# The second expert's weight load and the routing steps: another queue and another order

## The chip, the cores and the metric

One core of one Trainium2 chip runs the whole kernel. The metric is the device time of one launch in microseconds (us); lower is better.

## The reference

The input is 1024 tokens of 1024 channels, float32. A first layer adds a convolution-like attention with group norm. A second layer adds a 16-head causal attention and then a mixture of experts; the change lies in this last part. A layer norm is taken of every token, a gate picks experts, and each expert is one 1024 x 1024 product:

```python
gate_logits = softmax(x @ gate_w + gate_b, axis=-1)
selected = (gate_logits >= THRESHOLD)              # 0.1, 8 experts
weights = gate_logits * selected
weights = weights / where(sum(weights) == 0, 1, sum(weights))
for e in range(E):
    out = out + weights[:, e:e + 1] * (x @ expert_w[e] + expert_b[e])
```

What is returned is the token stream plus this sum.

## The kernel before

The tokens are eight tiles of 128 rows (`NT = 8`). The experts don't multiply every token: for each expert the kernel makes a list of the tokens that chose it, gathers their rows, multiplies them, scales them and adds them to the output with an accumulating DMA. Two experts, 0 and 7, are called short: for these the last tile of tokens isn't listed but multiplied in full, expert 0's share at the start ("the dense tile") and expert 7's at the end.

**Grouping, beside the attention's output projection.** The projection (`project_out`, L894) works through nine half tiles, each of eight products over 128 channels. After every product it calls `one_more` (L1373), which counts a "chunk" and issues the steps that the table `at_chunk` (L1326) lists for it. So the table is an order written out by hand: it says which small step follows which product. A step is `stage(n, t)` (L1306) for tile t:

- 0 `normalise` (L1116): layer norm of the rows; for tiles 0 to 5 the rows go to DRAM (L1129) and come back in quarters (L174), both by SP's queue.
- 1 `turn_rows` (L1139): VectorE transposes the quarters (L179); tiles 6 and 7 are transposed by TensorE (L1148) and copied by ScalarE (L1149).
- 2 `gate_sums` (L1158): TensorE products with the gate's weights (L1164), and a copy (L1168).
- 3 `gate` (L1174): products pg (L1179), maximum, exponential on ScalarE (L1191, L1194).
- 4 `thresholds` (L1197): ten small VectorE steps.
- 5 `place` (L1212): running counts `kept` (L1217), products pp (L1219, L1220), the place of each token (L1224 to L1230).
- 6 `entries_of` (L1233): comparisons `one` on VectorE (L1237) and products `entry` (L1245), which GpSimd makes for tiles 0 to 5 and VectorE for 6 and 7.
- 7 `enter` (L1254): TensorE products that add the entries to the lists (L1256).

Stages 2 to 5 run for a group of tiles at once: (0, 1, 2), (3, 4, 5), (6), (7). Each engine issues its steps in the order of the code inside such a stretch, so a step that waits holds back all later ones of its engine. The second table, `others` (L1364), holds what hangs on chunk numbers without being a stage; at chunks 43 and 65 ScalarE's queue loads the halves of expert 0's weights (`w0`).

**The dense tile and expert 0.** `weighted` (L1018) multiplies the last tile by expert 0's weights: two halves of eight products each (L1025), an addition of the bias on VectorE (L1028) and a scale on ScalarE (L1029). Its table `between` says what is issued after product (j, c), and after half j before that half's bias addition. In it come the last tile's stages 2 to 5, the transposes `put` of the gathered rows (L1457, L179), their sums `row_sums` (L1468, L152 to L155) and the sums of the weights, `first_sum` to `fourth_sum` (L1428 to L1442). GpSimd fetches rows by indirect DMA, four per row tile (`fetch`, L1006; L1010).

Then follows a loop over the experts (L1592). It loads the next expert's weights at its top (`load`, L1422: two halves of 2 MB by SP's queue, L121), and calls `products` (L1473) twice per expert, each for a pair of row tiles. That is a matrix product with seven block products in place of eight (L1487), numbered 0 to 6, with VectorE additions between them (L1495 to L1507). Its `between` hangs steps on these numbers. For expert 0, the last tile's stages 6 and 7 hang on product 2, `copy_lists` on 3 (L1264), and `last_lists` on 4 (L1400): products pc that spread the lists (L1276) and copies of them for all other experts (L1295 to L1298).

PSUM banks come from two sets of three, `mm` and `tr`; a product into a bank waits until its last content has been read.

Of the kernel before, what the change touches and what calls it, by code (L numbers as in the profile page):

```python
# [45 lines left out]
NT = TOK // P  # L46
# [10 lines left out]
E = 8  # L57
# [12 lines left out]
def kernel(  # L70
# [27 lines left out]
    nc = tc.nc  # L98
# [896 lines left out]
    w_even, t_pool = pool(weights, "w_even", 2), pool(weights, "t_pool")  # L995

    def half_weights(e, r, home, name="w_e", queue=nc.sync):

        return w_tile(f"{name}{e}_{r}", expert_w[e][:, ts(r, HALF)], home=home, queue=queue)
# [67 lines left out]
    with ExitStack() as gating:  # L1067
# [238 lines left out]
        def stage(n, t):  # L1306
            tiles = together[t]
            if n == 0:
                normal[t] = normalise(t)
            elif n == 1:  # L1310
                turned_rows[t] = turn_rows(t, normal[t])
            elif n == 2:
                summed[t] = gate_sums(tiles)
            elif n == 3:
                gated[t] = gate(tiles, summed[t])
            elif n == 4:
                gated[t] = thresholds(*gated[t])
            elif n == 5:
                placed[t] = place(tiles, *gated[t])
            elif n == 6:  # L1320
                entered[t] = entries_of(t, t - tiles[0], *placed[tiles[0]])
            else:
                enter(t, *entered[t])
# [6 lines left out]
            23: ((1, 1),),  # L1330
            27: ((0, 3),),
            30: ((1, 2),),
            33: ((2, 0),),
            34: ((0, 4),),
            36: ((3, 0),),
            38: ((1, 3), (4, 0)),
            42: ((5, 0), (6, 0)),
            44: ((6, 1),),
            46: ((7, 0), (6, 2)),
            47: ((1, 4),),  # L1340
            48: ((7, 1),),
            50: ((0, 5),),
            52: ((7, 2),),
            61: ((1, 5),),
            63: ((2, 3),),
            65: ((0, 6),),
            66: ((3, 3),),
            68: ((4, 3),),
            69: ((1, 6),),
            71: ((2, 6), (5, 3), (6, 3)),  # L1350
            73: ((3, 6), (6, 4)),
            75: ((7, 3), (4, 6), (6, 5)),
            76: ((7, 4),),
            77: ((5, 6), (6, 6)),
# [64 lines left out]
        w_odd, two = pool(pairs, "w_odd", 2, side="right"), pool(pairs, "two", 2, side="right")  # L1419
        w, bias, step, T, T3, A, S = {0: w0}, {0: bias0[0]}, {}, {}, {}, {}, {}  # L1420

        def load(e):  # L1422
            w[e] = [half_weights(e, r, w_odd if e % 2 else w_even) for r in range(2)]

        def half(e, j, l):
            return w[e][l][:, 4 * j : 4 * j + 4, :]
# [5 lines left out]
        def second_sum(e):  # L1432
            nc.vector.tensor_sub(T[e][1], half(e, 1, 1), T[e][0])  # L1433

        def bias_step(e):
            step[e] = two.tile([P, HALF], F32, tag="step", name=f"step{e}", bufs=1)
            nc.vector.tensor_sub(step[e], bias[e][:, HALF:], bias[e][:, :HALF])

        def fourth_sum(e):
            nc.vector.tensor_sub(T[e][2], half(e, 1, 0), T[e][1])  # L1440
# [16 lines left out]
        def put(e, k):  # L1457

            if k == last:
                A[e, k] = l2w.tile([P, NC, P], F32, tag="row_T", name=f"one{e}", bufs=3)  # L1460
                turn(A[e, k], row[e, k], LEFT)
            else:
                pair, i = divmod(k, 2)
                if i == 0:
                    A[e, pair] = two.tile([P, 2, NC, P], F32, tag="A", name=f"A{e}_{pair}")
                turn(A[e, pair][:, i, :, :], row[e, k])

        def row_sums(e, pair):  # L1468
            S[e, pair] = two.tile([P, 3, NC // 2, P], F32, tag="S", name=f"S{e}_{pair}")
            blocks = (A[e, pair][:, i, 4 * j : 4 * j + 4, :] for i in range(2) for j in range(2))  # L1470
            sums_of_A(*blocks, *(S[e, pair][:, i, :, :] for i in range(3)))
# [89 lines left out]
        with tc.manual_schedule():  # L1561
            entries, last_rows = [], []
            last_row_T = two.tile([P, NC, P], F32, tag="last_row_T", name="last_row_T", bufs=1)
            nc.scalar.copy(last_row_T, turned_rows[NT - 1])
            for k in range(3):
                get(0, k)
            y = weighted(
                lambda: gated[NT - 1][0][:, 0, 0, 1:2],
                turned_rows[NT - 1],
                w0,  # L1570
                bias0[0],
                l2w,
                "dense",
                {
                    (0, 2): lambda: stage(2, NT - 1),
                    (0, 4): lambda: (stage(3, NT - 1), first_sum(0)),
                    (0, 6): lambda: stage(4, NT - 1),
                    0: lambda: put(0, 0),
                    (1, 2): lambda: stage(5, NT - 1),
                    (1, 3): lambda: put(0, 1),  # L1580
                    1: lambda: (row_sums(0, 0), second_sum(0), bias_step(0)),
                },
            )
            get(0, 3)
            nc.gpsimd.indirect_dma_start(
                out=out,
                out_offset=bass.IndirectOffsetOnAxis(ap=token_i[:, NT - 1 : NT], axis=0),
                in_=y,
                in_offset=None,
                compute_op=ALU.add,  # L1590
            )
            for e in range(E):  # L1592
                if e % 2 == 0 and e:
                    left_over(e)
                if e + 1 < E:
                    load(e + 1)
                between = {
                    0: lambda: third_sum(e),
                    1: lambda: put(e, 2),
                    2: lambda: put(e, 3),  # L1600
                    4: lambda: row_sums(e, 1),
                }
                if e == 0:
                    between[2] = lambda: (stage(6, NT - 1), stage(7, NT - 1), fourth_sum(0), put(0, 2))
                    between[3] = lambda: (entries.append(copy_lists(1)), put(0, 3))
                    between[4] = lambda: last_lists(entries[0])
                    between.pop(1)
                elif e % 2:
                    between[0] = lambda: (third_sum(e), get(e, 3))
                    between[1] = lambda: (fourth_sum(e), put(e, 2))  # L1610
                if e % 2 == 0:
                    between[5] = lambda: (get(e + 1, 0), row_sums(0, 1) if e == 0 else None)
                    between[6] = lambda: get(e + 1, 1)
                elif e + 1 < E:
                    between[5] = lambda: (get(e, last), get(e + 1, last))
                    between[6] = lambda: get(e + 1, 0)
                products(e, 0, between)
                if e + 1 < E:
                    bias[e + 1] = expert_bias(e + 1, l2w, tag="xg", bufs=2)
                    between = {  # L1620
                        4: lambda: first_sum(e + 1),
                        5: lambda: second_sum(e + 1),
                        6: lambda: bias_step(e + 1),
                    }
                if e % 2 == 0:
                    between[1] = lambda: (put(e + 1, 0), get(e + 1, 2))
                    between[2] = lambda: put(e + 1, 1)
                    between[3] = lambda: row_sums(e + 1, 0)
                elif e + 1 < E:
                    between[1] = lambda: put(e, last)  # L1630
                    between[2] = lambda: (put(e + 1, last), sum_left(e))
                    between[3] = lambda: (put(e + 1, 0), get(e + 1, 1))
                else:
                    between = {
                        1: lambda: nc.sync.dma_start(last_rows[0], out[ts(NT - 1, P), :]),
                        4: lambda: nc.vector.scalar_tensor_tensor(
                            last_rows[0], bias[e], gated[NT - 1][0][:, 0, e, 1:2], last_rows[0], ALU.mult, ALU.add
                        ),
                    }
                products(e, 1, between)  # L1640


            for j in range(2):
                pe = mm(f"last_pe{j}")
                for c in range(NC):
                    nc.tensor.matmul(
                        pe, last_row_T[:, c, :], w[E - 1][j][:, c, :], start=(c == 0), stop=(c == NC - 1)
                    )
                y = last_rows[0][:, ts(j, HALF)]
                nc.vector.scalar_tensor_tensor(y, pe, gated[NT - 1][0][:, 0, E - 1, 1:2], y, ALU.mult, ALU.add)  # L1650
                nc.sync.dma_start(out[ts(NT - 1, P), ts(j, HALF)], y)
# [69 lines left out]
```

## Time and profile before

| | us |
|---|---|
| median of 3 runs | 1237.42 |
| lowest and highest run | 1237.3, 1238.69 |
| the profiled execution's own time | 1237.59 |
| its span, first to last instruction | 1235.8 |
| of it, to the start of the grouping | about 664 |
| grouping, to the dense tile's first product | 664 to 746.5 |
| dense tile | 746.5 to 761.3 |
| expert 0 | 761.3 to 809.6, and its last products to 816 |
| other experts and the end | to 1235.8 |

The profile is one execution, taken by the hardware profiler. PE is TensorE's matmul, PEld its weight load, DVE VectorE, ACT ScalarE, POOL GpSimd, SP the engine that issues most DMAs; a "q" behind an engine's name marks its sequencer, which issues DMAs. A float32 product shows as two matmuls. A row of the timeline gives start, duration, engine, line, operation, what is written and read, how often, and in brackets how long the engine had been idle before and what ended that. A list of waits gives who waited for whom, the total, the number of times and the longest. A DMA's own row is its issue; the trace also has the time at which its data landed. The granted TensorE clock was 1.000 throughout.

### The profile page before, as it was taken

The page shows a single profiled execution, that of the slowest core. Times are in us where ns is not written, and L with a number is a line of the kernel's source. Part 1 is how long each engine was busy: PE and PEld are TensorE (multiplying, and loading weights), DVE is VectorE, ACT ScalarE, POOL GpSimd, SP SyncE. Part 2 cuts the span into 40 slices and gives each one's busy share as a digit, 9 for nine tenths or more (in the row PEclk, how much of TensorE's full clock was granted, in tenths as well). Part 3 has the DMA queues.
Part 4 walks back from the last instruction along what each step waited for, and adds up shares of the span by engine and source line. Part 5 has one row for each costly group of instructions (what it writes and reads, how often), then busy time and mean ns, then how long its engine had stood idle before and what let it go on. Part 6 is the DMA issues. An engine that isn't in the chain of part 4 may idle for free.

```text
span 1235.8 us, 13219 instructions
## 1 busy us (share of the span) xinstructions
PE 1216.3 (98%) x4780; PEld 630.9 (51%) x4780; DVE 730.6 (59%) x1254; ACT 208.1 (17%) x502; POOL 410.1 (33%) x470
## 2 busy tenths in 40 slices
PE   9999999999999999999999999899999999999998
PEld 5445885778884444444444444444344434434443
DVE  5796636657333666657554656666656556565642
ACT  3310111120001222222221122101201111111110
POOL 0041341354000322223241116436452745364521
PEclk9999999999999999999999999999999999999999
DMA  9002014772210535353393747473855575556442
GB/s 349 23 1 80 6 50 140 240 254 69 68 47 23 167 107 166 105 172 103 114 291 113 232 171 255 88 219 89 239 146 155 111 230 164 147 143 180 100 83 54
DMA packets 94120, 169.76 MB, mean 137 GB/s; under 512 B 11968, under 2 KB 48848, under 8 KB 94048
## 3 DMA queue, kind: packets, MB, share of 16 engines
q1 hardware_dynamic: 75680, 112.68, 28.1%
q0 software_dynamic: 16144, 51.45, 17.3%
q10 hardware_dynamic: 2224, 4.72, 1.1%
q8 instruction: 39, 0.64, 0.2%
q14 instruction: 33, 0.27, 0.1%
HBM read 116.12 MB, written 48.50 MB: 133 GB/s over the span
## 4 chain that ended last, share of the span: by engine, by line
PE 67%; issue 13%; DMA 6%; POOL 6%; DVE 4%; SPq 2%; ACT 1%; DVEq 0%; POOLq 0%; ACTq 0%
PE p L1487 30%; PE pv L657 7%; POOL s_q L855 5%; PE pq_pair L392 4%; PE po L898 3%; PE left L1529 3%; PE pq L311 3%; PE pqk L657 3%; PE pk L423 2%; DMA ln_rows<-ln_rows 2%; PE pv L530 2%; PE rest L1543 2%; PE pT L502 2%; DMA quarters<-rows 1%; SPq L174 1%
## 5 line engine op out<-in xcount | busy, mean ns | idle before, releaser
L1010 POOL DMA_INDIRECT w_e_xg<-rows,gather x146 | 157.3, 1077 | 50.9 <-issue 41.1
L1487 PE MATMUL p<-w_e,A 128*128 128x512 f32 x368 | 163.2, 593 | 1.3 <-DVE slot L1297 1.3
L855 POOL TENSOR_TENSOR s_q<-s_q,total 128x128 f32<-128x128 f32 (+1 forms) x128 | 66.2, 548 | 276.8 <-DVE total L852 274.4
L1033 POOL DMA_INDIRECT out_dram<-y,add x32 | 57.4, 1795 | 177.3 <-ACT y L1493 111.1
L898 PE MATMUL po<-w_p,y_T 128*128 128x512 f32 x256 | 115.8, 601 | 0.0
L1487 PEld LDWEIGHTS p<-w_e,A 128*128 128x128 f32 x368 | 69.6, 190 | 89.9 <-issue 89.4
L1487 PE MATMUL p<-T,S 128*128 128x512 f32 x256 | 112.8, 593 | 0.4 <-DVE T L1433 0.4
L1493 ACT ACTIVATE y<-y,slot 128x512 f32<-128x512 f32 x64 | 46.0, 721 | 339.9 <-DVE y L1501 181.2
L841 ACT ACTIVATE s_q<-s,top 128x256 f32<-128x256 f32 (+1 forms) x128 | 56.6, 443 | 186.4 <-issue 147.0
L657 PE MATMUL pqk<-ln,w_qk 128*128 128x512 f32 x192 | 85.6, 595 | 0.0
L1487 PEld LDWEIGHTS p<-T,S 128*128 128x128 f32 x256 | 48.5, 190 | 61.6 <-issue 60.3
L898 PEld LDWEIGHTS po<-w_p,y_T 128*128 128x128 f32 x256 | 46.8, 190 | 52.3 <-issue 51.1
L179 DVE STREAM_TRANSPOSE A<-w_e_xg 128x1024 f32<-128x1024 f32 x32 | 39.7, 1239 | 52.4 <-DMA w_e_xg<-rows,gather 52.4
L657 PE MATMUL pqk<-T,S_qk 128*128 128x512 f32 x128 | 58.5, 599 | 0.0
L657 PEld LDWEIGHTS pqk<-ln,w_qk 128*128 128x128 f32 x192 | 36.0, 190 | 43.3 <-issue 42.3
L1487 PE MATMUL p<-T,A 128*128 128x512 f32 x128 | 57.5, 592 | 0.0
L1487 PE MATMUL p<-w_e,S 128*128 128x512 f32 x128 | 57.5, 592 | 0.0
L657 PE MATMUL pv<-w_v,ln 128*128 128x256 f32 x192 | 43.7, 380 | 2.3 <-ACT ln L215 1.1
L311 PE MATMUL pq<-w_q,xn 128*128 128x512 f32 x96 | 44.5, 599 | 0.3 <-ACT xn L291 0.3
L1529 PE MATMUL left<-w_e,one 128*32 128x512 f32 x312 | 41.8, 593 | 0.0
L657 PEld LDWEIGHTS pv<-w_v,ln 128*128 128x128 f32 x192 | 36.2, 190 | 7.9 <-ACT ln L215 1.3
L1487 PEld LDWEIGHTS p<-T,A 128*128 128x128 f32 x128 | 24.3, 190 | 30.6 <-issue 30.1
(328 smaller groups left out, 1849.9 us busy)
## 6 DMA issues: line engine op xcount, KB each, us to landing
w_e<-in_expert_w_dram SPq DMA_DIRECT2D x14, 2048.0 KB, 12.1
s_rows<-s_q SPq DMA_DIRECT2D x32, 384.0 KB, 2.3
s_rows<-s_rows SPq DMA_DIRECT2D x128, 96.0 KB, 2.4
w_qk<-in_W_attnT_dram SPq DMA_DIRECT2D x8, 1024.0 KB, 5.9
xn<-in_xT_dram SPq DMA_DIRECT2D x8, 512.0 KB, 7.2
w_q<-in_Wq_dram SPq DMA_DIRECT2D x16, 256.0 KB, 6.8
x_at<-in_x_dram POOLq DMA_DIRECT2D x8, 512.0 KB, 8.2
w_v<-in_W_attnT_dram SPq DMA_DIRECT2D x2, 2048.0 KB, 10.0
```

Of the source, the lines that this page charges most:

```text
L179: nc.vector.transpose(row_T[:, :, :slots].rearrange("p c (g j) -> p g c j", j=32), row[:, : slots // 32, :].rearrange("p g (c i) -> p g c ...
L311: nc.tensor.matmul(pq, xn[:, c, ts(t, P)], w_q[kc][:, c, :], start=(c == 0), stop=(c == NC - 1))
L392: nc.tensor.matmul(bank, a[:, c, :], b[:, c, :], start=(c == 0), stop=(c == NC // 2 - 1))
L657: nc.tensor.matmul(bank, stationary(c), moving(c), start=(c == 0), stop=(c == NC // 2 - 1))
L841: nc.scalar.activation(blocks(h, qt), s[:, h, cols].rearrange("p (b f i) -> p b f i", f=Q, i=32), AF.Exp, bias=top[:, qt, h : h + 1], accu ...
L855: nc.gpsimd.tensor_mul(blocks(h, qt), blocks(h, qt), total[:, qt, h : h + 1].unsqueeze(2).unsqueeze(3).to_broadcast([P, 1 + qt, Q, 32]),)
L898: nc.tensor.matmul(po, y_T[:, c, ts(t, P)], w_p[j][:, c, :], start=(c == 0), stop=(c == NC - 1))
L1010: nc.gpsimd.indirect_dma_start(out=row[:, g, :], out_offset=None, in_=table[: (TOK - P) * Q, :] if e in SHORT else table, in_offset=bass.I ...
L1033: nc.gpsimd.indirect_dma_start(out=out[: TOK - P, :] if e in SHORT else out, out_offset=bass.IndirectOffsetOnAxis(ap=add[:slots, e, k : k ...
L1487: nc.tensor.matmul(bank, a[:, c, :], b[:, c, :], start=(c == 0), stop=(c == NC // 2 - 1))
L1493: nc.scalar.mul(y[i][:, ts(j, HALF)], y[i][:, ts(j, HALF)], slot[:, e, 1, 2 * pair + i : 2 * pair + i + 1])
L1529: nc.tensor.matmul(bank[ts(i, 32), :], stationary, w[of][j][:, c, :], start=(c == 0), stop=(c == NC - 1))
```

## The change

Three things move; no step is added or removed.

1. `load` gets a parameter for the queue. Expert 1's weights are no longer loaded at the top of the loop by SP; they are loaded by ScalarE's queue, in the dense tile's step list after its second half's products (ahead of that half's bias addition and scale). The later experts' loads stay at the top of the loop, on SP.
2. The last tile's stage 5 follows the dense product (1, 1) instead of (1, 2), and its stage 6 comes with it instead of after expert 0's product 2.
3. In `at_chunk`, the stages of the two groups of three tiles and their neighbours come one or two chunks later, with some orders inside a chunk changed by that.

```diff
         at_chunk = {
...
-            33: ((2, 0),),
             34: ((0, 4),),
-            36: ((3, 0),),
-            38: ((1, 3), (4, 0)),
-            42: ((5, 0), (6, 0)),
-            44: ((6, 1),),
-            46: ((7, 0), (6, 2)),
+            35: ((2, 0),),
+            38: ((1, 3), (3, 0)),
+            40: ((4, 0),),
+            44: ((5, 0), (6, 0)),
+            46: ((6, 1),),
             47: ((1, 4),),
-            48: ((7, 1),),
-            50: ((0, 5),),
-            52: ((7, 2),),
+            48: ((7, 0), (6, 2)),
+            50: ((7, 1), (0, 5)),
+            53: ((7, 2),),
             61: ((1, 5),),
-            63: ((2, 3),),
-            65: ((0, 6),),
-            66: ((3, 3),),
-            68: ((4, 3),),
-            69: ((1, 6),),
-            71: ((2, 6), (5, 3), (6, 3)),
-            73: ((3, 6), (6, 4)),
+            65: ((2, 3), (0, 6)),
+            68: ((3, 3),),
+            69: ((4, 3), (1, 6)),
+            71: ((2, 6),),
+            72: ((5, 3), (6, 3)),
+            74: ((3, 6), (6, 4)),
             75: ((7, 3), (4, 6), (6, 5)),
...
-        def load(e):
-            w[e] = [half_weights(e, r, w_odd if e % 2 else w_even) for r in range(2)]
+        def load(e, queue=nc.sync):
+            w[e] = [half_weights(e, r, w_odd if e % 2 else w_even, queue=queue) for r in range(2)]
...
                     0: lambda: put(0, 0),
-                    (1, 2): lambda: stage(5, NT - 1),
+                    (1, 1): lambda: (stage(5, NT - 1), stage(6, NT - 1)),
                     (1, 3): lambda: put(0, 1),
-                    1: lambda: (row_sums(0, 0), second_sum(0), bias_step(0)),
+                    1: lambda: (row_sums(0, 0), second_sum(0), bias_step(0), load(1, nc.scalar)),
...
-                if e + 1 < E:
+                if 0 < e < E - 1:
                     load(e + 1)
...
-                    between[2] = lambda: (stage(6, NT - 1), stage(7, NT - 1), fourth_sum(0), put(0, 2))
+                    between[2] = lambda: (stage(7, NT - 1), fourth_sum(0), put(0, 2))
```

## The prediction

> All times are us of the profiled execution before (span 1235.8, own time 1237.59, which is 0.17 above the runs' median 1237.42); a sum made against it is subtracted from the median.
>
> **What bounds the kernel now.** First the page's busy shares, then TensorE's own waits.
>
> ```profile
> PE 1216.3 (98%) x4780; PEld 630.9 (51%) x4780; DVE 730.6 (59%) x1254; ACT 208.1 (17%) x502; POOL 410.1 (33%) x470
> ```
>
> TensorE is busy for 1216.3 of 1235.8: the change neither adds nor removes a product, so it can only be worth idle TensorE time, 19.5 us in all. Next, the list of waits for TensorE from 620 to 800, where everything touched lies (line waited for: us in total, times, longest).
>
> ```profile
> PE lists L1256 <- DVE entry L1245: 2.6, 1, 2.6
> PE parts L1164 <- DVE row_T L179: 1.8, 2, 1.1
> PE p L1487 <- DVE slot L1297: 1.3, 1, 1.3
> PE pp L1220 <- DVE kept L1217: 0.6, 2, 0.4
> PE pc L1276 <- DVE entries L1267: 0.5, 1, 0.5
> PE p L1487 <- DVE T L1433: 0.4, 1, 0.4
> PE lists L1256 <- POOL entry L1245: 0.3, 1, 0.3
> ```
>
> That is the whole prize: 1.8 + 0.6 + 0.3 = 2.7 in the grouping (665 to 743), 2.6 + 0.4 + 1.3 in the dense tile and first expert. What leads to the 2.6 and 0.4 is read from the timeline (start, us, engine, line; idle before it).
>
> ```profile
> 748.25 0.49 SPq L121 DMA_DIRECT2D w_e<-in_expert_w_dram  x1
> ...
> 756.92 0.96 POOL L1010 DMA_INDIRECT w_e_xg<-rows,gather  x1 [0.30 <-issue]
> ...
> 759.32 0.17 DVE L1230 TENSOR_SCALAR at<-at 128x8 int32<-128x8 int32 x1
> ...
> 762.94 1.25 DVE L179 STREAM_TRANSPOSE A<-w_e_xg 128x1024 f32<-128x1024 f32 x1 [3.45 <-DMA w_e_xg<-rows,gather]
> ...
> 769.21 3.70 PE L1487 MATMUL p<-T,S 128*128 128x512 f32 x8 [0.44 <-DVE T L1433]
> ...
> 773.88 0.75 DVE L1237 TENSOR_TENSOR one<-count,at 128x256 f32<-128x256 int32 x2
> 774.66 0.76 DVE L1245 TENSOR_TENSOR entry<-one,listed 128x256 f32<-128x256 f32 x2
> ...
> 775.48 0.42 PE L1256 MATMUL lists<-entry,one 128*32 128x64 f32 x12 [2.56 <-DVE entry L1245]
> ```
>
> VectorE has the last tile's places at 759.49, then idles 3.45 until the gather of the second row tile lands; from 762.94 to 775.4 it never rests, with the entries (1.5 us) at the end of that queue and TensorE waiting for them. The gather was late because the DMA engines were full (stretches: us, busy times, clock, DMA share, GB/s).
>
> ```profile
> 750.00:762.00 12.00, 12.00 (x33) 5.72 (x33) 7.26 (x24) 1.02 (x2) 9.26 (x10) 1.00 1.04 396
> 762.50:774.00 11.50, 9.98 (x23) 3.91 (x21) 10.86 (x12) 0.73 (x2) 8.86 (x6) 1.00 0.24 74
> ```
>
> Gathers issued in the first stretch land 5.8 to 7.1 us later (median 5.9); those issued from 763.2 to 766 land in 2.7 to 3.0. What fills the engines is expert 1's weights: halves issued by SP at 742.15 and 748.25, landing 8.8 and 13.2 later.
>
> [...] a DMA's window leaves the data movement out. The trace agrees: 0.96 shown, 2.7 to 7.1 to landing, so I use landings. [...] Here a gather issue takes 2.44 instead of 0.96 at 752.91, beside the 2.28 us difference of L1430; I keep that cost.
>
> **The change, part by part.**
>
> *Load of expert 1.* Leaves SP at 742.15 and 748.25; on ScalarE it stands behind the scale of the dense tile's first half (758.41), so it is issued at about 758.4: two issues, 0.42 and 0.37 by the ScalarE weight loads at 693 and 725. Behind them on ScalarE waits only the second half's scale (770.40): 10 us of cover. Its buffers were free by 748.25, as the old issue shows. On SP, the row write (742.88), the grouped rows (747.87) and the bias (748.82) no longer queue with it; nobody waits for these early. The gather issued at 756.92 should then land 2.9 later, at 759.8, not 762.81. New cost: 4.2 MB at 396 GB/s is 10.6 us, landing by about 771; its first reader is the sum at 809.3 (38 us of cover). Gathers of the third and fourth row tile (last issues 761.96 and 767.49) now run beside it: at 5.9 to 7.1 they land by 769 and 775, wanted by the moved-up transposes at 774.2 and 776.2. Nothing.
>
> *Entries of the last tile.* 0.75 + 0.76 = 1.5 us go from after 773.88 to 759.5, into the idle 3.45. The place step goes one product earlier (756.15 instead of 757.01); its input is ready at 755.34, so no wait. VectorE then reaches the transpose at max(761.0, 759.8) = 761.0: 1.94 earlier than 762.94. The T sum ends at 769.16 − 1.94 = 767.2; TensorE wants it at 769.21 − 0.44 = 768.77. The 0.44 goes, with 1.6 to spare. The list products then wait for nothing: 2.56 goes. Either half of this pair would nearly suffice: the move of the entries alone frees 2.56; the load alone brings the entries some 3 us earlier. *What is late next:* third sum 768.3 to 770.6, first two results to 772.0, fourth sum to 774.2, transposes and results to 778.7; product 4 ends at 779.4 and needs none of them late. Then the spreading of the lists (pc) and its copies: the 1.3 at L1297 is a round trip TensorE, VectorE, TensorE and stays. **Dense stage: −3.0.**
>
> *Groups.* A chunk is one po product, 0.86 (7.06 / 8). Gate sums of tiles 0 to 2 move from chunk 33 to 35: 687.05 to 688.77; tile 2's transpose ends 688.70: the 0.61 goes. Sums of 3 to 5 from 63 to 65: 1.14 goes. Now the new waits.
> - The gate of the first group comes behind tile 3's transpose, which ends at 695.46 (DMA). Four small steps of 0.2, Exp, then from the threshold's first step to pp took 2.97 (695.38 to 698.35): 696.55 + 2.97 = 699.5. TensorE is there at 698.9: 0.6 instead of 0.35. Costs 0.25. No table load is added; the same two surround this Exp.
> - ScalarE's load of w0 (issued 693.43) sits behind that Exp, so goes to about 696.3. Tile 4's row write then has 3 us for itself (it took 6.35 beside the load, 3.64 without), and the quarters, issued 696.7 to 698.1, land about 703.5 to 704.5 beside it. Tile 4's transpose now stands ahead of tile 2's entries: landing + 1.3 + 0.75, then GpSimd 1.2: 707 to 708; TensorE wants them at 708.8. Nothing, by 1 us.
> - After chunk 65 TensorE stands 1.7 earlier than before. Place step of tiles 3 to 5: one chunk after the sums of tile 6, so its 0.36 goes, and VectorE's chain starts 1.42 earlier (729.8, not 731.22). That chain (entries of 3, 4, 5, thresholds of 6 between) is what TensorE meets next: entries of 4 at 735.1 against TensorE at 734.3 (two chunks now, three before), entries of 5 at 738.35 against 737.9. About 1.25 of waits, in place of 0.28. So the end of this stage moves by the chain's 1.4, not by 2.3. The last statistics, transposes and dense products hang on it unchanged.
>
> **Groups: −1.4**; bounds 0 (tile 4 late, chain not earlier) and −2.6 (no new wait).
>
> Sum: −1.4 − 3.0 = −4.4: 1237.59 − 4.4 = 1233.2, and from the median **1233.0**, 0.36% faster.
>
> **The rivals.**
> - *The groups give nothing*: tile 4's quarters land after 706, or the chain's steps stretch beside GpSimd (one took 0.55 instead of 0.2 at 735.98). Then only the dense stage: 1237.4 − 3.0 = 1234.4. For it: margins of 1 us. Against: two visible waits go.
> - *A wait takes the place of the 2.56*: the list products start early, but products 3 to 5 wait for bank copies in VectorE's full queue (busy 10.86 of 11.5). Only the groups' 1.4 remains: 1236.0. Against: my replay leaves VectorE idle from 778.7.
> - *The load stays early in effect*, or the gather is as late as before: transposes at 762.94, but entries already done; −1.4 − 2.56: 1233.5, inside the forecast.
> - *Slower*: tile 4's row write and quarters are served behind the whole w0 load (696.3 + 10.4 = 706.7). Every us that the quarters land after 705.4 delays tile 2's entries, and tile 5's rows after them; at 709.8 it has eaten all 4.4. Row write at 706.7, quarters issued to 708.1, landing 3.3 later: 711.4, so 1.6 beyond that: 1239.0. For it: a bias queued with the weights took 14.5. Against: the same quarters beside the same load took 5.2 to 5.5.
>
> **How the numbers follow.** Forecast (with the late-gather case) 0.64 at 1233.0, own range 1231.8 to 1234.0; groups nothing 0.17 at 1234.4; replaced wait 0.12 at 1236.0; slower 0.07 at 1239.0. Low end: all 5.6 of removable waits (2.6 + 3.0), 1231.8. High end 1236.2 takes in the third case. About 0.2%, 2.5 us, is what a measurement of this kernel can tell from no change: faster takes the forecast and most of the second case, 0.78; same 0.15; slower 0.07.
>
> **What would show it.** Right: no wait at L1256 for VectorE's entry near 775, none at L1433; gathers of the second row tile landing in about 3 us; the transpose near 761 less the groups' shift; L1297 still 1.3; parts at L1164 without wait; new waits of about 0.8 and 0.5 at L1256 for GpSimd's entries. Wrong: a wait at L1487 on another VectorE result before product 5; tile 4's quarters landing after 706; weights of expert 1 issued well before or after 758.

## The result and the profile after

| | before | after |
|---|---|---|
| median of 12 runs each, same chip | 1237.89 | 1234.05 |
| lowest to highest | 1234.49 to 1241.5 | 1231.97 to 1237.01 |
| profiled execution, own time | 1237.59 | 1232.3 |
| its span | 1235.8 | 1230.4 |

The ratio is 0.9969 with an interval of 0.9956 to 0.9982: the changed kernel is faster by 0.31%, 3.84 us. Since two profiled executions can differ by nearly as much for other reasons, the spans are first cut at marks that both kernels have (us):

| stretch | before | after | difference |
|---|---|---|---|
| start to the attention's last product (nothing changed here) | 664.34 | 663.07 | −1.27 |
| grouping: from there to the dense tile's first product | 82.13 | 81.42 | −0.71 |
| dense stage: to expert 0's product 5 | 39.04 | 35.71 | −3.33 |
| expert 0's rest, other experts, end | 450.26 | 450.24 | −0.02 |

The first row is no effect of the change: over the thirteen profiles of this study it lies between 660.75 and 664.34, with the same code in all. What the change did is the sum of the next two, −4.04, beside −3.84 in the medians. The forecast had −1.4 for the groups and −3.0 for the dense stage, so the total hides one step that was right and one that wasn't.

The page's busy shares of the kernel after:

```profile
PE 1214.7 (99%) x4780; PEld 631.6 (51%) x4780; DVE 729.9 (59%) x1254; ACT 207.9 (17%) x502; POOL 408.3 (33%) x470
```

As before 4780 products; TensorE's idle time is 1230.4 − 1214.7 = 15.7, where it was 19.5. TensorE's waits from 660 to 800, after (lines behind the table `at_chunk` now have numbers lower by 2: L1485 is the product, L1431 the T sum):

```profile
PE lists L1256 <- POOL entry L1245: 2.2, 3, 1.3
PE p L1485 <- DVE slot L1297: 1.3, 1, 1.3
PE pc L1276 <- DVE entries L1267: 0.5, 1, 0.5
PE dense_pe L1025 <- ACT row_T L1149: 0.2, 1, 0.2
```

Gone are the 2.6 for VectorE's entry, the 0.4 for T, the 1.8 at L1164 and the 0.6 at L1220. But the last row of before, 0.3 for GpSimd's entries, has become the first, 2.2 in three waits: in the grouping 2.7 stood before and 2.2 stand now.

The dense stage in the timeline after:

```profile
756.43 1.01 ACTq L121 DMA_DIRECT2D w_e<-in_expert_w_dram  x2
...
757.33 0.17 DVE L1230 TENSOR_SCALAR at<-at 128x8 int32<-128x8 int32 x1
...
757.45 0.78 DVE L1237 TENSOR_TENSOR one<-count,at 128x256 f32<-128x256 int32 x2
...
758.27 0.76 DVE L1245 TENSOR_TENSOR entry<-one,listed 128x256 f32<-128x256 f32 x2
...
758.94 1.24 DVE L179 STREAM_TRANSPOSE A<-w_e_xg 128x1024 f32<-128x1024 f32 x1
...
766.63 3.60 PE L1485 MATMUL p<-T,S 128*128 128x512 f32 x8
...
770.16 0.42 PE L1256 MATMUL lists<-entry,one 128*32 128x64 f32 x12
```

The stage starts 1.98 earlier than before (744.49 against 746.47). VectorE no longer idles ahead of the transpose: places, entries and transpose follow one another, and the transpose starts at 758.94 (761.0 less 1.98 had been forecast, 759.0). The second row tile's last gather, issued at 754.92, had landed by 757.70, in 2.8. Product 2 (766.63) and the list products (770.16) have no bracket: they waited for nothing. The weights are issued at 756.43 (forecast 758.4 less 1.98) and fill the DMA engines a stretch later than before:

```profile
748.50:760.50 12.00, 12.00 (x34) 5.68 (x33) 9.87 (x28) 1.02 (x2) 9.56 (x9) 1.00 0.48 141
760.50:772.00 11.50, 11.50 (x39) 5.03 (x38) 11.33 (x11) 1.44 (x2) 8.09 (x6) 1.00 1.05 380
```

(Stretch, length, busy TensorE, weight load, VectorE, ScalarE, GpSimd, clock, DMA share, GB/s.) In the second, all 11.50 of TensorE's time are busy, where before it was 9.98.

The grouping after, around tile 2's entries:

```profile
691.70 0.34 SPq L1129 DMA_DIRECT2D rows<-row  x1
...
694.62 0.42 ACTq L121 DMA_DIRECT2D w_e<-in_expert_w_dram  x1
...
695.11 1.93 SPq L174 DMA_DIRECT2D quarters<-rows  x4
...
705.22 1.25 DVE L179 STREAM_TRANSPOSE row_T<-quarters 128x1024 f32<-128x1024 f32 x1 [4.22 <-DMA quarters<-rows]
...
706.39 0.72 DVE L1237 TENSOR_TENSOR one<-count,at 128x256 f32<-128x256 int32 x2
...
707.25 1.20 POOL L1245 TENSOR_TENSOR entry<-one,listed 128x256 f32<-128x256 f32 x2 [4.61 <-DVE one L1237]
...
708.50 0.43 PE L1256 MATMUL lists<-entry,one 128*32 128x64 f32 x16 [1.29 <-POOL entry L1245]
```

Read upward from the last row: TensorE stood 1.29 for GpSimd's entries, GpSimd for VectorE's comparisons, VectorE 4.22 for tile 4's quarters, and these were issued 0.5 behind the first half of expert 0's weights. They landed 5.8, 6.9, 7.8 and 8.6 after their issues, the last at 705.10. In the kernel before, the quarters landed no earlier (706.67), but tile 2's entries stood ahead of that transpose, so the lateness reached nobody:

```profile
703.87 1.20 POOL L1245 TENSOR_TENSOR entry<-one,listed 128x256 f32<-128x256 f32 x2 [0.76 <-DVE one L1237]
...
706.80 1.25 DVE L179 STREAM_TRANSPOSE row_T<-quarters 128x1024 f32<-128x1024 f32 x1 [3.07 <-DMA quarters<-rows]
...
708.48 0.43 PE L1256 MATMUL lists<-entry,one 128*32 128x64 f32 x16
```

### The profile page after: what moved, and what is told of

Same layout as the page of the kernel before. It is cut to its first block, busy times and chain, and to the rows that moved or that the text cites. A ratio compares the mean times of both kernels' runs of the same rounds, so it can differ in the third digit from the quotient of the medians.

```text
span 1230.4 us, 13216 instructions
## 1 busy us (share of the span) xinstructions
PE 1214.7 (99%) x4780; PEld 631.6 (51%) x4780; DVE 729.9 (59%) x1254; ACT 207.9 (17%) x502; POOL 408.3 (33%) x470
## 4 chain that ended last, share of the span: by engine, by line
PE 68%; issue 13%; DMA 7%; POOL 5%; SPq 3%; DVE 2%; ACT 1%; POOLq 0%; DVEq 0%; ACTq 0%
PE p L1485 31%; PE pv L657 7%; POOL s_q L855 5%; PE po L898 4%; PE pq_pair L392 4%; PE left L1527 3%; PE pq L311 3%; PE pqk L657 3%; DMA ln_rows<-ln_rows 3%; PE pk L423 2%; PE rest L1541 2%; PE pv L530 2%; PE pT L502 2%; SPq L479 2%; DMA quarters<-rows 1%
## 5 line engine op out<-in xcount | busy, mean ns | idle before, releaser
L1485 PE MATMUL p<-w_e,A 128*128 128x512 f32 x368 | 163.2, 593 | 1.3 <-DVE slot L1297 1.3
L1485 PEld LDWEIGHTS p<-w_e,A 128*128 128x128 f32 x368 | 69.7, 190 | 89.8 <-issue 89.8
L1485 PE MATMUL p<-T,S 128*128 128x512 f32 x256 | 112.7, 593 | 0.0
L1485 PEld LDWEIGHTS p<-T,S 128*128 128x128 f32 x256 | 48.6, 190 | 60.7 <-issue 60.7
L1485 PE MATMUL p<-T,A 128*128 128x512 f32 x128 | 57.5, 592 | 0.0
L1485 PE MATMUL p<-w_e,S 128*128 128x512 f32 x128 | 57.5, 592 | 0.0
L1485 PEld LDWEIGHTS p<-w_e,S 128*128 128x128 f32 x128 | 24.4, 190 | 30.6 <-issue 29.9
L1485 PEld LDWEIGHTS p<-T,A 128*128 128x128 f32 x128 | 24.4, 190 | 30.6 <-issue 30.3
```

What stands on the lines that cost most here:

```text
L1485: nc.tensor.matmul(bank, a[:, c, :], b[:, c, :], start=(c == 0), stop=(c == NC // 2 - 1))
```

## The experiments

The theory after this result: the dense stage gives what was forecast, for the reason given; the groups give less because tile 4's transpose is in front of tile 2's entries and its quarters are served beside expert 0's load. The rival: the groups' waits went as forecast, and the new ones are small variations of DMA. The runs were made on three chips, on which the kernel before has medians of 1237.5 (e1 to e4), 1237.69 (e5 to e8) and 1236.63 (e9 to e11).

**The three parts alone, and the first two together.** *e1* has only this of the change:

```diff
-            w[e] = [half_weights(e, r, w_odd if e % 2 else w_even) for r in range(2)]
+            w[e] = [half_weights(e, r, w_odd if e % 2 else w_even, queue=queue) for r in range(2)]
...
-                    1: lambda: (row_sums(0, 0), second_sum(0), bias_step(0)),
+                    1: lambda: (row_sums(0, 0), second_sum(0), bias_step(0), load(1, nc.scalar)),
...
-                if e + 1 < E:
+                if 0 < e < E - 1:
```

> Only expert 1's weight load goes to ScalarE's queue behind the dense tile; groups and entries stay as before. Theory (either half alone takes most of the dense stage's waits): the gather of the second row tile lands about 2.9 us after its issue instead of 5.9, its transpose starts near 759.8 instead of 762.9 (times of the profile before), everything on VectorE comes some 3 us earlier, so TensorE's wait for the entries falls from 2.6 to at most 0.3 and the 0.4 at the T sum goes: the stretch from the dense tile's first product to expert 0's product 5 falls from 39.04 to about 36 us; time ratio 0.9975. Rival (the two moves add up, the load is worth only the 0.4): the stretch is 38.6 us, and the wait of about 2.6 for the entries is still there.

*e2* has only the places and entries:

```diff
-                    (1, 2): lambda: stage(5, NT - 1),
+                    (1, 1): lambda: (stage(5, NT - 1), stage(6, NT - 1)),
...
-                    between[2] = lambda: (stage(6, NT - 1), stage(7, NT - 1), fourth_sum(0), put(0, 2))
+                    between[2] = lambda: (stage(7, NT - 1), fourth_sum(0), put(0, 2))
```

> Only the last tile's stages 5 and 6 move into the dense tile; load and groups stay as before. Theory: the gather still lands 5.9 us after its issue and the transpose still starts near 763, so the 0.4 at the T sum stays, but the entries are made in VectorE's idle 3.45 us, so the 2.6 goes: the stretch from the dense tile's first product to expert 0's product 5 is 36.4 us (39.04 before); time ratio 0.9978. Rival (the late gather is what holds the lists, whatever the place of the entries): a wait of 2 us or more in front of products 2 to 5 stays, stretch 38.5 us or more.

*e3* has the new `at_chunk` table alone, in full as in the change:

```diff
-            38: ((1, 3), (4, 0)),
+            38: ((1, 3), (3, 0)),
+            40: ((4, 0),),
...
-            63: ((2, 3),),
-            65: ((0, 6),),
+            65: ((2, 3), (0, 6)),
...
```

> Only the table of the routing groups changes; the dense stage stays as before. Theory (tile 4's quarters beside expert 0's first half load hold back tile 2's entries): TensorE waits about 1.3 us for GpSimd's entries of tile 2 and about 1 us for those of tiles 4 and 5; the stretch from the last attention product to the dense tile's first product falls from 82.13 to about 81.4 us, the dense stage stays at 39.0; time ratio 0.9994. Rival (the forecast on record: groups give 1.4): 80.7 us, no wait for tile 2's entries.

*e4* has the diffs of e1 and e2 together and keeps the old table:

```diff
-                    (1, 2): lambda: stage(5, NT - 1),
+                    (1, 1): lambda: (stage(5, NT - 1), stage(6, NT - 1)),
...
+                    1: lambda: (row_sums(0, 0), second_sum(0), bias_step(0), load(1, nc.scalar)),
```

> Load and entries move, the groups' table stays as before. Theory: stretch from the dense tile's first product to expert 0's product 5 35.7 us as in the changed kernel, grouping 82.1 us as before; time ratio 0.9973, less than the sum of the two moves alone (2.6 + 3.0 us). Rival (the two moves add up or help each other beyond the 3.0 us of waits): more than 3.5 us less than before.

Measured (stretches from each profile, us; "before" has the stretches of its one profile and the median on this chip; the ratio is an estimate from the runs of both kernels on that chip, not the quotient of the two medians):

| | grouping | dense stage | median | ratio and interval |
|---|---|---|---|---|
| before | 82.13 | 39.04 | 1237.5 | |
| e1, load alone | 82.15 | 36.12 | 1233.38 | 0.997 (0.9959 to 0.9981) |
| e2, entries alone | 82.46 | 36.39 | 1232.28 | 0.9968 (0.9956 to 0.998) |
| e4, both | 82.38 | 35.71 | 1231.48 | 0.9959 (0.9946 to 0.9972) |
| e3, groups alone | 83.39 | 39.00 | 1237.4 | 1.0005 (0.9997 to 1.0013) |

The load alone takes 2.92 from the dense stage, the entries alone 2.65, both 3.33: not a sum of two gains but two ways to take away one wait. TensorE's waits from 760 to 800 in e1:

```profile
PE p L1487 <- DVE slot L1297: 1.3, 1, 1.3
PE lists L1256 <- DVE entry L1245: 0.3, 1, 0.3
```

and in e2:

```profile
PE p L1487 <- DVE slot L1297: 1.3, 1, 1.3
PE p L1487 <- DVE T L1433: 0.4, 1, 0.4
```

With the load alone the gathers come early and the whole VectorE queue with them: T's wait goes and 0.3 of the 2.6 is left. With the entries alone the gathers are as late as before (5.9 from issue to landing beside the load) and T's 0.4 stays, but the entries are out of that queue. Each leaves a rest that the other one takes. In the times e4 gains more than was expected of it (0.9973); more on that below.

The groups alone change nothing in the time that could be measured, with both signs in the interval, and lose 1.26 in the grouping of their profile, where 81.4, a wait of 1.3 and a ratio of 0.9994 had been expected. Its waits from 660 to 800, the rows of the grouping:

```profile
PE lists L1256 <- POOL entry L1245: 3.9, 3, 3.0
...
PE pp L1220 <- DVE kept L1217: 0.4, 1, 0.4
```

The 1.8 at L1164 is gone here too. In its place stands one wait of 3.00 for tile 2's entries: tile 4's quarters, issued 0.4 behind the load, took 6.0 to 10.5 and the last landed at 705.66. So in this profile the groups cost something, and the rival (small variations) doesn't carry a wait of 1.3 and of 3.0 at the same place.

**The cause and the way out.** *e5* is the changed kernel, with the first half of expert 0's weights on SP's queue, where its issue comes behind tile 4's quarters:

```diff
-            43: lambda: w0.append(half_weights(0, 0, w_even, queue=nc.scalar)),
+            43: lambda: w0.append(half_weights(0, 0, w_even)),
```

> The changed kernel, but the first half of expert 0's weights (chunk 43) is loaded by SP instead of ScalarE, so it stands behind tile 4's quarters on SP's queue. Theory (that load beside the quarters is what makes the groups worth so little): the quarters land about 3.3 us after their issue (8.6 in the changed kernel), TensorE's wait of 1.3 us for tile 2's entries goes, the stretch from the last attention product to the dense tile's first product falls from 81.4 to 80.1 to 80.4 us, near the 80.7 of the forecast on record; dense stage 35.7 as in the changed kernel. Rival (the quarters are late because of their own row write and the output rows, or VectorE's order holds the entries anyway): quarters still over 5 us, wait of about 1 us stays, stretch 81 us or more.

*e6* is the changed kernel with products 5 and 6 of expert 0's first call in the other set of banks, to see what the 1.3 at L1297 is:

```diff
-                bank = (tr if n % 2 else mm)(f"p{n}_{name}")
+                bank = (tr if (n + (e == 0 and pair == 0 and n > 4)) % 2 else mm)(f"p{n}_{name}")
```

> The changed kernel, but products 5 and 6 of expert 0's first pair swap their bank sets, so product 5 no longer needs the bank of the spread lists. Theory (the 1.3 us before product 5 is the wait for that bank, from TensorE over VectorE's copies back to TensorE): the wait at L1297 goes and no other takes its place, the stretch from the dense tile's first product to expert 0's product 5 falls from 35.7 to 34.4 us, everything after it as before; time ratio to the kernel before 0.996. Rival (VectorE's copies hold back the next additions, so the wait moves behind product 5 or 6): the stretch to product 5 is shorter, but the next one, to the first left-over product (79.13), is longer by as much.

*e7* is the changed kernel with the list products (stage 7) of tiles 3, 4 and 5 a chunk later (an entry of the table is stage, tile), to see whether the waits for the entries of tiles 4 and 5 cost or only stand where VectorE's chain is awaited anyway:

```diff
-            75: ((7, 3), (4, 6), (6, 5)),
-            76: ((7, 4),),
-            77: ((5, 6), (6, 6)),
-            78: ((7, 5),),
+            75: ((4, 6), (6, 5)),
+            76: ((7, 3),),
+            77: ((5, 6), (6, 6), (7, 4)),
+            79: ((7, 5),),
```

> The changed kernel, but the list products of tiles 3, 4 and 5 come one chunk later (76, 77 and 79 in place of 75, 76 and 78). Theory (VectorE's chain of thresholds and entries sets the end of the grouping, TensorE's waits of 0.5 and 0.4 in it are cover): these two waits go, but the stretch from the last attention product to the dense tile's first product stays as in the changed kernel with the same landing of tile 4's quarters (waits for tile 2's entries taken off: 80.1 us), within 0.2. Rival (TensorE's waits add up to the end): 0.9 us less.

*e8* has the edits of e5 and e6:

```diff
-            43: lambda: w0.append(half_weights(0, 0, w_even, queue=nc.scalar)),
+            43: lambda: w0.append(half_weights(0, 0, w_even)),
...
-                bank = (tr if n % 2 else mm)(f"p{n}_{name}")
+                bank = (tr if (n + (e == 0 and pair == 0 and n > 4)) % 2 else mm)(f"p{n}_{name}")
```

> The changed kernel with both mends: expert 0's first half load behind the quarters, and the swapped banks. Theory: 80.2 us for the grouping and 34.4 for the dense stage, together 2.6 us less than in the changed kernel: time ratio to the kernel before about 0.9945. Rival: the two don't add up, ratio 0.996 or more.

| | grouping | dense stage | median | ratio and interval |
|---|---|---|---|---|
| before | 82.13 | 39.04 | 1237.69 | |
| e5, load behind the quarters | 80.21 | 35.71 | 1230.32 | 0.9944 (0.9928 to 0.996) |
| e6, other bank | 85.08 | 34.25 | 1233.36 | 0.9959 (0.9947 to 0.9971) |
| e7, list products later | 85.99 | 37.42 | 1235.64 | 0.9987 (0.9974 to 1.0) |
| e8, e5 and e6 | 80.43 | 34.25 | 1230.28 | 0.9943 (0.9924 to 0.9963) |

e5 settles the cause. Tile 2's entries and tile 4's transpose in its timeline:

```profile
693.52 1.74 SPq L174 DMA_DIRECT2D quarters<-rows  x4
...
695.78 0.43 SPq L121 DMA_DIRECT2D w_e<-in_expert_w_dram  x1
...
699.41 1.23 DVE L179 STREAM_TRANSPOSE row_T<-quarters 128x1024 f32<-128x1024 f32 x1
...
701.89 1.20 POOL L1245 TENSOR_TENSOR entry<-one,listed 128x256 f32<-128x256 f32 x2 [0.76 <-DVE one L1237]
...
705.63 0.43 PE L1256 MATMUL lists<-entry,one 128*32 128x64 f32 x16
```

The transpose has no wait at all, the entries are ready 2.5 ahead of TensorE, and the grouping is 1.92 shorter than before, 1.21 shorter than in the changed kernel. The load itself still lands at 706.35, 10.6 after its issue; its first reader is the dense tile's first product, 35 later. In e8, the other kernel with this edit, the one quarter that can be seen took 2.93, there is no wait for tile 2's entries, and the grouping is 80.43. e5 moved the load to another queue and to a later time at once; which of the two is needed was not tried.

e5's is the lowest ratio but for e8's: 0.56% ahead of the kernel before. e6 and e8 differ in this load alone and ran on one chip: 1233.36 beside 1230.28, though both scatter by 5 us and more. e5's interval overlaps the changed kernel's (0.9956 to 0.9982, and 0.9974 to 0.999 in e9) only at the edge of the first. It also overlaps e4's, so that the mended groups gain over the old table is shown by the grouping of the traces, not by the medians.

e6 shows that the 1.3 is nothing but a bank that must be read before product 5 writes into it. Product 5 follows the spreading of the lists without a bracket:

```profile
780.20 1.05 PE L1276 MATMUL pc<-entries,copies 128*128 128x64 f32 x8
...
781.46 3.68 PE L1485 MATMUL p<-w_e,A 128*128 128x512 f32 x8
```

The dense stage is 1.46 shorter with no step moved, and from product 5 to the first left-over product it is 79.14 as in the changed kernel (79.13), so the wait has not gone elsewhere. In the medians the gain can't be told apart: e8 beside e5 is 1230.28 beside 1230.32. e6's profile and e7's also show the wait for tile 2's entries, with 2.97 and 2.81. Of 22 runs, e6 has nine from 1228.5 to 1230.3 and thirteen from 1232.5 to 1236.8. More on both is in the last section.

e7 is inconclusive on the size. The waits for the entries of tiles 4 and 5 did shrink (one is 0.24, the other gone), but those for tile 6's entries (0.40) and for expert 0's list (0.88) grew by as much: the last three waits of the grouping are 0.50 + 0.43 + 0.54 = 1.47 in the changed kernel and 0.24 + 0.40 + 0.88 = 1.52 in e7. So they seem to stand where VectorE's chain is awaited anyway, as the prediction had it. The 85.99 itself can't tell: beside the wait of 2.81 it holds two stretches in which the clock was halved (last section), and the expected 80.1 is met only by an estimate, 85.99 less 2.81 less about 1.7 for each stretch, 79.8. And e7's dense stage became 1.7 longer than the changed kernel's, with a copy of the last tile's sums (L1168) that started 2.2 after its products; why it was late stays open.

**The change and its dense part again, side by side, and the wait filled.** *e9* is the changed kernel itself and *e10* is e4 once more, for one comparison on one chip:

```diff
-                    (1, 2): lambda: stage(5, NT - 1),
+                    (1, 1): lambda: (stage(5, NT - 1), stage(6, NT - 1)),
```

(This diff and the load are in both; the table is in e9 alone.)

> The changed kernel once more, beside the next two on one chip, for a second profile of its grouping. Theory (what the groups' table is worth depends on when tile 4's quarters land beside expert 0's load): wait for tile 2's entries between 1 and 3 us, grouping between 81.2 and 83.5 us (82.1 to 82.5 with the old table); median 2 us above the kernel with the load and entries alone. Rival (forecast on record: the groups give 1.4): grouping 80.7, median 1.4 below that kernel.

> Load and entries moved, the groups' table of before, beside the changed kernel on the same chip. Theory: grouping 82.1 to 82.5 us, dense stage 35.7, time ratio to the kernel before 0.996 to 0.9973, not above that of the changed kernel. Rival: above the changed kernel's by 0.001.

*e11* is the changed kernel with 14 matmuls that nobody reads, put where TensorE stands for tile 2's entries. They are added work; nothing is left out:

```diff
+            elif n == 8:
+                fill = tr("fill")
+                for _ in range(7):
+                    nc.tensor.matmul(fill[:, :P], before, ones, start=True, stop=True)
...
-            53: ((7, 2),),
+            53: ((8, 2), (7, 2)),
```

> The changed kernel with seven 128x128 products into a bank that nobody reads (about 1.8 us of TensorE), ahead of tile 2's list products, where TensorE waits for its entries. Theory (a stretch of 3.4 us at half the clock follows that wait in some executions because TensorE stood still for about 3 us): with the fillers at most 1.2 us are stood still, no half-clock stretch near 710 us, few runs more than 3 us above the fastest, median not above the changed kernel's although up to 0.5 us of products may be too much. Rival (the half-clock stretches have nothing to do with that wait): a stretch at half the clock in the same place, the same spread of the runs, and the median up to 0.5 us higher.

| | grouping | dense stage | median | ratio and interval |
|---|---|---|---|---|
| e9, changed kernel | 84.42 | 35.71 | 1234.09 | 0.9982 (0.9974 to 0.999) |
| e10, load and entries alone | 81.84 | 35.71 | 1230.82 | 0.996 (0.9946 to 0.9974) |
| e11, wait filled | 83.23 | 35.71 | 1233.24 | 0.9969 (0.9954 to 0.9984) |

The dense stage is 35.71 in all three, and the groups' table is all in which e9 and e10 differ: 3.27 in the medians, 2.58 in the grouping of the profiles. The two intervals just touch, so a cost of the groups is likely on this chip and its size is open. e9's grouping is longer than the expected 81.2 to 83.5. e11 shortens the wait from 2.83 to 1.51 (1.2 had been expected) and has no half-clock stretch behind it (last section), but its interval holds e9's median, and three of its seven runs are more than 3 above its fastest, where few had been expected.

## Why the prediction was right and where it was wrong

The time, 1234.05, came 1.05 above the forecast: right in sign and inside the whole range, just above the 1234.0 at which the range of the main case ends. That it came so near owes something to luck: the dense stage gave more than was said, and the groups, for which 1.4 was counted, gave 0.71 in a profile that is the best of four; on another chip (e9) the whole change gave 0.18% in place of 0.31%. By its steps:

**Dense stage, −3.0 forecast, −3.33 measured.** Right, as a mechanism and in the places, and mis-sized by 0.33, which lie at the same two waits: from product 1 to 2 it is 0.60 less than before, from 2 to 3 2.73 less, where the idle times of 0.44 and 2.56 had been counted. The transpose is at 758.94, there is no wait at T and none at the list products, there are 1.46 to spare at product 2 (T's sum ends at 765.17) where 1.6 was said, and L1297 is still 1.3. Right too was "Either half of this pair would nearly suffice" (e1, e2). The later steps that were named as the next that could be late (third and fourth sum, products 3 and 4) waited for nothing, and product 5 for its old 1.3 alone, so the rival of a wait that takes the place of the 2.56 falls; so does the case of a gather as late as before.

**The load's collision, "Nothing".** Right: the gathers of row tiles 2 and 3 took 5.8 to 7.7 beside the load, the last landed at 772.77, and the transposes at 772.13 and 774.07 waited for none of them. The load fills the DMA engines alike from SP (396 GB/s at a share of 1.04, first stretch before) and from ScalarE (380 GB/s at 1.05, second after). The load was moved to where its neighbours have time, not made cheaper. One reading was wrong without harm: of the gathers issued in the first stretch before, 5.8 to 7.1 holds for those up to 756.92; the next four, from 758.18 to 761.96, took 5.4, 4.4, 3.6 and 2.8, as the load neared its landing at 761.49.

**Groups, −1.4 forecast.** Wrong. The changed table has four profiles with it in place and nothing else altered in the grouping: 81.42 (after), 83.39 (e3), 84.42 (e9), 85.08 (e6). The old table has five: 82.13, 82.15, 82.46, 82.38, 81.84. The means are 83.6 and 82.2: in these traces it costs 1.4 on average in place of giving it. About 1.7 each of e9 and e6 are a stretch at half the clock (last section); without these the mean is 82.7, still no gain. In the times it costs 0.6 by e3's ratio (1.0005 × 1237.5, with both signs in the interval) and 3.3 by the medians of e9 and e10. The forecast stated bounds of 0 and −2.6; the first profile's −0.71 lies between them, the mean doesn't.

The step that failed is this one: "the quarters, issued 696.7 to 698.1, land about 703.5 to 704.5 beside it. ... Nothing, by 1 us." Its order was right, its issue times nearly (1.26 is the shift of the kernel's start: 694.62 is 695.9 in before's times, where 696.3 was said), and its term mis-sized: 5.4 to 6.4 for the last quarter beside the load, where 8.6 (after) and 10.5 (e3) were measured. e5, with the load behind them, has 2.95 for the one whose landing its trace holds. The 5.2 to 5.5 had been read from the kernel before, where the load was 6.7 us old when the quarters were issued. In the changed kernel they follow it by 0.5, when at the 396 GB/s seen, by estimate, at most 0.2 of its 2 MB can have moved: here a transfer's time beside another depended on how much of the other was left. Two rows of before showed it: the gathers named above, quicker as the load ran out, and the bias issued 0.57 behind a load, which took 14.5 and which the prediction quoted only for its slower rival.

The other terms of the groups came true in kind: waits of 0.50 and 0.43 for the entries of tiles 4 and 5 (0.8 and 0.5 forecast), the first group's pp wait under 0.2 in the changed kernel, 0.29 in e5 and 0.40 in e3 (0.6 forecast). Two figures on the way were slips that the −1.4 doesn't rest on: the 0.35 that the 0.6 was set against is the second group's wait (the first's was 0.23), and the 2.3 that TensorE would gain leaves out the 0.25 charged to that wait. With the quarters out of the way, e5's −1.92 lies between the forecast's −1.4 and its bound of −2.6: the reading of the order was sound, and the one transfer spoiled it.

**The rivals.** "The groups give nothing", with quarters landing after 706, is the one whose sign came true, in before's times 705.10 + 1.26 = 706.4; it forecast 1234.4 and 1234.05 was measured. The slower one (quarters behind the whole load, landing at 711.4) falls in its size but was right on the place and the point from which it decides: a wait of 1.29 for quarters at 706.4 and, in e3, of 3.00 for quarters at 708.3 (both in before's times) point to 705.1 and 705.3 as the landing without a wait, and 705.4 had been said.

**What the profiles don't explain.** By their ratios (0.9959 and 0.996) e4 and e10 gain about 5; their grouping and dense stage together gain 3.1 and 3.6 in the profiles. The near ends of the intervals are 3.5 and 3.2, so most of each interval lies beyond. (By the medians the gains are 6.0 and 5.8. e4's rival, more than 3.5, so fits its times and not its stretches.) Part of it goes with the mean granted clock, which was measured for each run: in 67 of the 101 runs of the kernel before on the three chips it is 0.998 or less, in e4 and e10 in one of twelve. Beside only those runs of before that have 0.999 or more, e4's median is 4.8 ahead and e10's 4.6. The profile of before is of the rarer kind, and what lowers the clock in the others no trace shows; the last section names a candidate. With one profile of each and 3.6 of spread in the unchanged start, where the rest comes from stays open. The changed kernel's two ratios, 0.9969 and 0.9982, agree within their intervals.

## What to carry to other kernels

A transfer's duration read from a trace held here only for the same distance to the load beside it (the quarters took 5.2 to 5.5 beside a load 6.7 old, 5.8 to 8.6 beside one 0.5 old): before you move a small urgent transfer, see how old the large one will be at its issue, and put the large one behind it if nobody needs it soon (in e5, on the same queue). Where two causes end in one wait, either cure can take most of the gain, as in e1 (2.92 of 3.33) and e2 (2.65), so don't add them. And a step that is moved in front of another on a queue lends it its own waits: tile 2's entries had nothing to do with tile 4's DMA until they stood behind its transpose, and TensorE then stood 1.29 for them.

## What the runs showed of the hardware

A wait of TensorE of nearly 3 us can cost more than itself. In e9 TensorE stood 2.83 at tile 2's entries, and the granted clock then fell (columns as above; the clock is the third number from the end):

```profile
707.48:707.87 0.39, 0.39 (x17) 0.30 (x17) 0.39 (x1) 0.00 (x0) 0.00 (x0) 1.00 0.00 0
707.87:711.28 3.41, 3.41 (x8) 1.49 (x5) 0.70 (x5) 1.44 (x2) 0.00 (x0) 0.50 0.05 19
711.28:714.00 2.72, 2.72 (x8) 1.21 (x7) 0.69 (x1) 0.00 (x0) 0.00 (x0) 1.00 0.43 172
```

and in e6, after 2.97:

```profile
709.53:710.08 0.55, 0.55 (x17) 0.46 (x18) 0.52 (x2) 0.00 (x0) 0.00 (x0) 1.00 0.00 0
710.08:713.49 3.41, 3.41 (x5) 1.35 (x5) 0.56 (x4) 1.44 (x2) 0.00 (x0) 0.50 0.10 38
713.49:715.00 1.51, 1.51 (x5) 0.68 (x4) 0.53 (x1) 0.00 (x0) 0.00 (x0) 1.00 0.65 260
```

In both the products resume at the full clock, and 0.39 and 0.55 later one stretch of 3.41 at half the clock begins; e7 has one too (0.50 from 710.32 to 713.73), 0.71 after a wait of 2.81. Such a stretch costs about 1.7: the twelve products of the projection behind the wait, which take 10.50 in the changed kernel's first profile, took 12.19 in e6 and in e7. After a wait of 3.00, e3 has no such stretch (1.00 from 702 to 718; its twelve products took 10.49), so the length of the wait alone doesn't decide; what else does, these traces don't show. Nor is there one (1.00 from 702 to 718) after the shorter waits of the changed kernel's first profile (1.29) and of e11 (1.51, with 1.72 of matmuls ahead of it), or in e4 and e5, which don't wait for tile 2's entries.

Nor does each such stretch stand behind a wait of that length. e7 has another:

```profile
744.46:747.87 3.41, 3.41 (x18) 3.41 (x17) 2.37 (x11) 1.69 (x3) 0.63 (x1) 0.50 0.95 303
```

The waits just ahead of it are 0.40 (to 742.49) and 0.88 (to 743.80). What set this one off stays open. Time at half the clock also stands behind the last product, where TensorE has no more work: 0.82 in before's profile (from 1234.98) and 3.40 in after's (from 1227.00), both at 0.50.

The clocks of the single runs carry the finding further than one trace of each kernel. By an estimate from the traces, a stretch of 3.41 at half the clock takes 1.7 of some 1232 from a run's mean clock, about 0.0014. Of e6's 22 runs the nine faster ones all have 0.999 or 1.000, and eleven of the thirteen slower ones 0.997 or 0.998. On one chip, 12 of e9's 18 runs have 0.998 or less, and none of the seven of e11, in which the wait is filled. Over all experiments it is 53 of 84 runs in the kernels whose profile shows a wait of 2.5 or more (e3, e6, e7, e9), and 4 of 47 in the others (3 of 12 in the first runs of the changed kernel). Where in a run the clock fell is known only for those with a trace.

The kernel before belongs to the first kind: 67 of its 101 runs on the three chips have 0.998 or less, and their medians are 2.0 to 2.4 above those of the rest. Its one long wait is the 2.56 at the list products. In the profile there is no stretch behind it (1.00 from 664 to 780). That this wait is followed by such a stretch in other runs, and that the change removed it too, would fit these clocks, but no trace shows it.
